# Attention and feed-forward block: first tokens' norm on VectorE, another order in the k and q products, the first codes loaded two units sooner, the last products by halves of a block

## The chip, the core and the metric

The kernel runs on one core of a Trainium2 chip. The core has five engines that run side by side, each with its own queue of instructions: TensorE (PE, matrix products into PSUM, the accumulation memory), VectorE (DVE), ScalarE (ACT), GpSimd (POOL) and SyncE (SP), which here only issues DMA transfers. PE loads its 128x128 stationary operand with an instruction of its own (PEld), which can run beside the product before. The metric is device time in microseconds (us), the median of several runs.

## The reference

The input x is 16 sequences of 256 tokens with 256 features each, 4096 tokens in all. Two steps follow each other:

```python
x = x + layernorm(attention(layernorm(x)))     # 16 heads of 128 features, causal
x = x + layernorm(ffn(layernorm(x)))           # 2048 hidden features
```

Attention projects the normed tokens to q, k and v with biases, takes a causal softmax over 256 keys, and multiplies by an output matrix. The feed-forward step is gelu(gate) times up, and then a down product; its three weight matrices come as 4-bit codes, two in an integer, with one scale for 32 codes, and have to be unpacked. Everything is float32.

## The kernel before

**Arithmetic.** A product of two float32 matrices is made of three products of a faster form: each operand is split into a high part (a copy rounded to that form) and a low part (what the rounding left), and high x high, low x high and high x low are summed in PSUM. `mm3` (line 353) writes such a group. With two slices of the inner dimension a group has six matmuls. `MOVING_LAST` fixes the order inside a slice: high weights with the high moving operand, low weights with the high moving operand, high weights with the low moving operand. ScalarE makes high parts, VectorE or GpSimd low parts.

**Order of work.** All instructions go through `run` (line 95), which keeps the written order on each engine, and all transfers go through `dma` (line 86) to the one queue of SP, also in written order. So an instruction that waits holds everything written later on its engine. Side work (splitting of weights, unpacking of codes, norms) is written as Python generators. `slot` (line 133) runs one step of the first of them that may run at this place, from six lists in a fixed order; `finish` runs a list to its end.

**Start.** `first_tokens` (line 245) loads the first block of 512 tokens in two halves, measures mean and variance (`ln_stats`, line 155: VectorE sums, and a power of -1/2 on GpSimd), norms the tokens, turns them with eight 128x128 transposes on PE (tile `tpx`, four for each half), and splits them into high (`scalar.copy`) and low (`vector.tensor_tensor`) parts in the tile `xT`. VectorE norms the first half, ScalarE the second. Between these, `w_split` (line 298) splits the first k and q weights. PE does 24 transposes of a constant matrix (tile `warm`, line 937) while the first loads are under way. After `first_tokens` the first two v weights are split, with low parts by GpSimd; both are needed for the first v product, which multiplies by four heads at once.

**Attention.** A unit is one head of one block of 512 tokens; there are 8 blocks and 16 heads, so 128 units. The loop of line 952 is a pipeline: in iteration i it does scores and softmax of unit i+3 (`st_s`, tiles `sc` and `pr`), the k and q products of unit i+4 (`st_qk`, tiles `pk` and `pq`), the way of the softmax through DRAM that transposes it (`hop`, `pt`), the product with v (`pz`), the v product (`pv`) and the output product (`po`). In `st_s` VectorE's list of written work holds one slot between the softmax of the two sequences, from which the unpacking of the feed-forward codes can run. In iterations with even i and head pair g (two units a pair), lines 954 to 965 start other work: at block 0, pair 7 (iteration 14) `f_load` issues the first two transfers of codes and scales (`ld`, tag `raw`), and 24 unpacking jobs (`f_make`, line 598) go onto the list `idle`. Each `f_make` issues the loads for the next one in its second step.

**Feed-forward.** The loop of line 1008 goes over 32 groups: 4 pairs of blocks (1024 tokens) times 8 slices of the hidden dimension. In a group, gate and up are computed with seven products in place of eight (`m1` to `m7`, class `Two`, tiles `pa`, `pd`, `pf`, `pe`). `pd`, `pf` and `pe` share the two PSUM buffers of the tag `sc`. Element-wise work goes onto the list `pending`, in a fixed order for ScalarE and VectorE: add, gelu, multiply, high part, low part, for each of four quarters of the group. `part` (line 830) runs one or two of these operations after each product, and `quarter` (line 841) runs as many as a down product needs. The down products of a group (`st_d`, line 850, tile `pd<-inter,wd`) are written among the products of the next group, six matmuls of 512 tokens each, block 1 first. They add up in four PSUM tiles over the eight groups of a pair of blocks.

**End.** Since the last group has no next one, the loop runs once more for its down products alone. Each of the last two blocks goes through `end_now` (line 897): ScalarE copies the two sums (`oT`), PE turns them by eight transposes (`tpo`), `ln_stats` measures 512 tokens, ScalarE and VectorE norm two tiles of 128 tokens each (`fa`), VectorE adds the residual (`xs`) and SP issues the output in two transfers.

Of the kernel before, what the change touches and what calls it, by code (L numbers as in the profile page):

```python
# [18 lines left out]
P = 128  # L19
# [3 lines left out]
NG = 8  # L23
# [5 lines left out]
def kernel(  # L29
# [215 lines left out]
    def first_tokens():  # L245

        xs = [x_load(x, 0, hf) for hf in range(2)]
        yield V_
        stats = []
        for hf in range(2):  # L250
            stats.append((yield from ln_stats([xs[hf][:, t, :] for t in range(2)])))
        w_split(0, "k")
        xn = wide("xn")
        nb = ln_shift(*stats[1], 2)
        for t in range(2):
            mv, rs = stats[0]
            run(
                nc.vector.tensor_scalar,
                xn[:, t, :], xs[0][:, t, :], mv[:, t, 0:1], rs[:, t : t + 1], ALU.subtract, ALU.mult,
            )  # L260
        for t in range(2):
            ln_apply_act(xn[:, 2 + t, :], xs[1][:, t, :], nb, stats[1][1], t)
        w_split(0, "q")
        xt = XT[1, 0] = work.tile([P, 2, 2, TB], F32R, tag="xT", name="xT", bufs=4)
        for hf in range(2):
            tp = ps.tile([P, 2, S], F32, tag=("pk", "pq")[hf], name="tpx")
            for kt in range(2):
                for t in range(2):
                    run(
                        nc.tensor.transpose,  # L270
                        tp[:, kt, t * P : (t + 1) * P], xn[:, 2 * hf + t, kt * P : (kt + 1) * P], ident,
                    )
            cols = slice(hf * S, (hf + 1) * S)
            hi, lo = xt[:, 0, :, cols], xt[:, 1, :, cols]
            run(nc.scalar.copy, hi, tp)
            run(nc.vector.tensor_tensor, lo, tp, f(hi), ALU.subtract)
        ready.add((1, 0))


# [18 lines left out]
    def w_split(p, n):  # L298

        raw = RAW.pop((p, n)).rearrange("p (k c) -> p k c", k=2)  # L300
        key, done = p, True
        if n == "v":
            key, done = p // 2, p % 2
            w = HALF.pop(key) if done else w_tile(n)
            if not done:
                HALF[key] = w
            wv_ = w_view(w)[:, :, :, (p % 2) * 256 : (p % 2 + 1) * 256]
        else:
            w = w_tile(n)
            wv_ = w_view(w)  # L310
        c = qscale if n == "q" else 1.0
        run(nc.scalar.activation, wv_[:, 0], raw, AF.Copy, scale=c)
        if n in "vo":
            run(nc.gpsimd.tensor_tensor, wv_[:, 1], raw, f(wv_[:, 0]), ALU.subtract)
        else:
            run(nc.vector.scalar_tensor_tensor, wv_[:, 1], raw, c, f(wv_[:, 0]), ALU.mult, ALU.subtract)
        ahead = p + (2 if n == "v" else 1)
        if ahead < NG:
            w_raw(ahead, n)
        if done:  # L320
            W[key, n] = w_view(w)
            late.append((now[0] + 4, w_keep, (key, n, w)))
# [27 lines left out]
    MOVING_LAST = ((0, 0), (1, 0), (0, 1))  # L350
    STATIONARY_LAST = ((0, 0), (0, 1), (1, 0))

    def mm3(o, terms, passes=STATIONARY_LAST, start=True, stop=True, shared=False):

        todo = [(lhs(a), rhs(c)) for lhs, rhs in terms for a, c in passes]
        for i, (lhs, rhs) in enumerate(todo):
            run(
                nc.tensor.matmul, o, lhs, rhs, start=start and i == 0, stop=stop and i == len(todo) - 1, skip_group_check=shared
            )
# [9 lines left out]
    def st_qk(i):  # L369
# [9 lines left out]
        mm3(pk, [(lambda a, kt=kt: wk_[:, a, kt, cols], lambda c, kt=kt: xt[:, c, kt, :]) for kt in range(2)], MOVING_LAST)  # L379
# [7 lines left out]
        K[i] = (kh, kl, kr)  # L387

        pq = ps.tile([P, TB], F32, tag="pq", name="pq")
        mm3(pq, [(lambda a, kt=kt: wq_[:, a, kt, cols], lambda c, kt=kt: xt[:, c, kt, :]) for kt in range(2)], MOVING_LAST)  # L390
# [459 lines left out]
    def st_d(k, bb, dh):  # L850


        if not 0 <= k < NGRP:
            return
        sb, g = divmod(k, NG)
        b = 2 * sb + bb
        w = FW[k, "d"]
        tags = (("po0", "po1"), ("pv", "pz"))[bb]
        if g == 0:
            ACC[b, dh] = ps.tile([P, TB], F32, tag=tags[dh], name="pd")  # L860
        po = ACC[b, dh]
        cols = slice(dh * P, (dh + 1) * P)
        i = [quarter(k, c, bb) for c in range(2)]
        mm3(
            po, [(lambda a, c=c: w[:, a, c, cols], lambda s, c=c: i[c][:, s]) for c in range(2)], MOVING_LAST,
            start=g == 0, stop=g == NG - 1, shared=True,
        )
        if g == NG - 1:
            if sb < NSB - 1:
                if dh == 0:  # L870
                    ACC[b] = back_tile()
                back(ACC[b], dh, po)
                if dh == 1:
                    add((urgent, behind)[bb], end(b, ACC.pop(b)), N_)
            else:
                if dh == 0:
                    ACC[b] = wide("oT").rearrange("p a b -> p (a b)").rearrange("p (h n) -> p h n", h=2)
                run(nc.scalar.copy, ACC[b][:, dh], po)
                if dh == 1:
                    add(urgent, end_now(b, ACC.pop(b), tags), V_)  # L880

    def end(b, tr):
        o = yield from back_load(tr)
# [10 lines left out]
        for hf in range(2):  # L894
            dma(half(out, b, hf), X1[b][hf])

    def end_now(b, oT, tags):

        yield V_
        tp = []  # L900
        for hf in range(2):
            tp.append(ps.tile([P, 2, D], F32, tag=tags[hf], name="tpo"))
            for t in range(2):
                for dh in range(2):
                    run(
                        nc.tensor.transpose,
                        tp[hf][:, t, dh * P : (dh + 1) * P], oT[:, dh, (2 * hf + t) * P : (2 * hf + t + 1) * P], ident,
                    )
        o = [tp[t // 2][:, t % 2, :] for t in range(4)]
        mv, rs = yield from ln_stats(o)  # L910
        nb = ln_shift(mv, rs, 4)
        fa = wide("fa")
        for t in range(2):
            ln_apply_act(fa[:, t, :], o[t], nb, rs, t)
        for t in range(2, 4):
            run(
                nc.vector.tensor_scalar,
                fa[:, t, :], o[t], mv[:, t, 0:1], rs[:, t : t + 1], ALU.subtract, ALU.mult,
            )
        for hf in (1, 0):  # L920
            run(nc.vector.tensor_tensor, X1[b][hf], X1[b][hf], fa[:, 2 * hf : 2 * hf + 2, :], ALU.add)
            dma(half(out, b, hf), X1[b][hf])


    first = first_tokens()
# [26 lines left out]
    for i in range(-4, N + 2):  # L952
        p = i // 2
        odd = i % 2 == 1
        if p >= 0 and not odd and p < len(pairs):
            b, g = pairs[p]
            if g == 0 and b + 1 < NBLK:
                add(urgent, ln1(b + 1), N_)
            if b == 0 and g == 7:
                pieces = [(fg, n) for fg in range(NG) for n in "gud"]  # L960
                f_load(*pieces[0])
                for m, piece in enumerate(pieces):
                    add(idle, f_make(*piece, pieces[m + 1] if m + 1 < len(pieces) else None), V_)
            if b == NBLK - 1 and g == 0:
                add(spare, x_ops(0), N_)
# [39 lines left out]
            part(k, name)  # L1005

    X[0].pop("last")()
    for k in range(NGRP + 1):
        sb, g = divmod(k, NG)
        if k < NGRP:  # L1010
            if g == 2 and sb + 1 < NSB:
                while not {(0, 2 * sb + 2), (0, 2 * sb + 3)} <= ready:
                    step(behind)
                add(spare, x_ops(sb + 1), N_)
            if g == NG - 1:
                for b in (2 * sb, 2 * sb + 1):
                    X1[b] = [x_load(x1d, b, hf, ("pr", "tr")[b % 2]) for hf in range(2)]
        if k > 0:
            parts(k, "m1", "m2")
        st_d(k - 1, 1, 0)  # L1020
# [22 lines left out]

_OUTS = [((NT, D), "float32")]
# [48 lines left out]
```

## Time and profile before

| what | value |
|---|---|
| median of three runs | 1543.86 us (1541.33 to 1545.67) |
| the profiled execution | 1548.52 us; its span in the trace 1546.7 us, the rest lies around it |
| mean granted TensorE clock | 0.991 |
| matmuls and weight loads | 7792 and 7792 |
| one unit in the steady part of the attention | 7.83 to 7.84 us from one `sc` start to the next |
| one group of the feed-forward | 14.96 us (1493.25 to 1508.21 us) |
| first `pk` matmul | at 10.87 us |
| first `sc` matmul | at 16.44 us |
| last matmul of the gate and up products ends | some 0.4 us after 1521.58 us |

How to read it: the profile is one execution with times from the start of its span. In a row of the timeline the first number is the start of the first instruction, the second the time from there to the end of the last one, both in us, and xN says how many follow each other. What stands in brackets is how long the engine sat idle before and what ended that. Rows of matmuls overlap at their ends, since products are pipelined, so for their pace starts are compared. "SPq" rows are the issuing of a transfer and not the transfer itself. A table of windows gives busy time of the engines in a stretch, with the number of instructions, then the granted TensorE clock as a fraction of full speed, the busy share of the DMA engines and GB/s. Nearly all instructions carry line 99, the line of the helper `run`, so tiles' names tell them apart.

### The profile page before, as it was taken

The page shows a single profiled execution, that of the slowest core. Times are in us where ns is not written, and L with a number is a line of the kernel's source. Part 1 is how long each engine was busy: PE and PEld are TensorE (multiplying, and loading weights), DVE is VectorE, ACT ScalarE, POOL GpSimd, SP SyncE. Part 2 cuts the span into 40 slices and gives each one's busy share as a digit, 9 for nine tenths or more (in the row PEclk, how much of TensorE's full clock was granted, in tenths as well). Part 3 has the DMA queues.
Part 4 walks back from the last instruction along what each step waited for, and adds up shares of the span by engine and source line. Part 5 has one row for each costly group of instructions (what it writes and reads, how often), then busy time and mean ns, then how long its engine had stood idle before and what let it go on. Part 6 is the DMA issues. An engine that isn't in the chain of part 4 may idle for free.

```text
span 1546.7 us, 25648 instructions
## 1 busy us (share of the span) xinstructions
PE 1510.8 (98%) x7792; PEld 1281.4 (83%) x7792; DVE 1178.4 (76%) x2944; ACT 1033.0 (67%) x2600; POOL 810.1 (52%) x1017
## 2 busy tenths in 40 slices
PE   8999999999999999999999999989999999999996
PEld 7888888888888888888888888877788878878884
DVE  6875878788788788878777777847777777787765
ACT  6876667767767676676675777656666665665663
POOL 3754669568667767766866866861420330240100
PEclk9999999999999999999999999989999999999999
DMA  8998899989899999899899889975547456655551
GB/s 276 335 310 257 249 303 302 313 293 300 280 293 317 291 310 296 267 326 309 266 315 294 287 281 322 324 238 204 216 179 275 185 220 212 236 192 214 218 195 42
DMA packets 200411, 407.55 MB, mean 263 GB/s; under 512 B 21457, under 2 KB 128465, under 8 KB 189521
## 3 DMA queue, kind: packets, MB, share of 16 engines
q1 hardware_dynamic: 200272, 405.91, 78.6%
q8 instruction: 62, 1.02, 0.3%
q14 instruction: 77, 0.62, 0.1%
HBM read 294.15 MB, written 111.67 MB: 262 GB/s over the span
## 4 chain that ended last, share of the span: by engine, by line
PE 80%; DMA 6%; DVE 5%; ACT 4%; SPq 2%; issue 1%; POOL 0%; DVEq 0%; POOLq 0%; ACTq 0%
PE pd L99 11%; PE po L99 10%; PE pk L99 10%; PE pv L99 10%; PE pq L99 9%; PE pz L99 9%; PE sc L99 8%; PE pa L99 7%; PE pf L99 5%; DVE sum L99 3%; DMA wo<-wo 2%; PE pe L99 2%; SPq L91 2%; ACT inter L99 1%; DMA hop<-tr 1%
## 5 line engine op out<-in xcount | busy, mean ns | idle before, releaser
L99 POOL TENSOR_SCALAR pr<-pr,rc 128x128 f32<-128x128 f32 (+1 forms) x512 | 251.7, 508 | 80.8 <-DVE rc L99 80.8
L99 POOL TENSOR_TENSOR pl<-pt,ph 128x512 fp32r<-128x512 f32 x128 | 165.3, 1291 | 218.3 <-ACT ph L99 211.8
L99 ACT ACTIVATE pr<-sc,mn 128x128 f32<-128x128 f32 (+1 forms) x512 | 208.9, 421 | 83.1 <-DVE mn L99 81.7
L99 DVE CUSTOM_DVE_ANT_0 sc<-sc,mask 128x128 f32<-128x128 f32 (+1 forms) x512 | 180.7, 373 | 63.5 <-PE sc L99 54.7
L99 PE MATMUL pv<-wv,xT 128*128 128x512 f32 x768 | 208.9, 407 | 0.0
L99 PE MATMUL pd<-inter,wd 128*128 128x512 f32 x768 | 199.5, 393 | 5.2 <-ACT inter L99 4.0
L99 PE MATMUL pk<-xT,wk 128*128 128x512 f32 x768 | 201.5, 398 | 1.6 <-ACT wv L99 1.4
L99 PE MATMUL pq<-xT,wq 128*128 128x512 f32 x768 | 196.4, 391 | 0.0
L99 ACT ACTIVATE zh<-pz,bqk 128x512 fp32r<-128x512 f32 x128 | 88.5, 692 | 160.6 <-PE pz L99 160.6
L99 POOL TENSOR_TENSOR rs<-rs,mhalf 128x4 f32<-128x4 f32 (+1 forms) x33 | 35.1, 1065 | 288.5 <-DVE rs L99 287.2
L99 PEld LDWEIGHTS pd<-inter,wd 128*128 128x128 f32 x768 | 142.3, 188 | 42.5 <-DVE inter L99 7.0
L99 PEld LDWEIGHTS pq<-xT,wq 128*128 128x128 f32 x768 | 144.5, 188 | 32.9
L99 PE MATMUL po<-zh,wo 128*128 128x512 f32 x512 | 160.3, 394 | 8.4 <-DMA wo<-wo 8.4
L99 PEld LDWEIGHTS pk<-xT,wk 128*128 128x128 f32 x768 | 136.5, 190 | 25.5 <-ACT xT L99 1.6
L99 PEld LDWEIGHTS pv<-wv,xT 128*128 128x128 f32 x768 | 135.0, 189 | 23.6
L99 DVE SCALAR_TENSOR_TENSOR zl<-pz,bqk,zh 128x512 fp32r<-128x512 f32 x128 | 95.2, 744 | 76.9 <-ACT zh L99 76.7
L99 ACT COPY part<-pa 128x512 f32<-128x512 f32 x192 | 111.9, 586 | 62.4 <-PE pa L99 59.8
L99 ACT CAST inter<-sum 128x512 fp32r<-128x512 f32 x128 | 80.1, 626 | 101.1 <-DVE sum L99 100.9
L99 DVE TENSOR_TENSOR inter<-sum,inter 128x512 fp32r<-128x512 f32 x128 | 92.1, 720 | 58.9 <-ACT inter L99 56.0
L99 DVE STREAM_TRANSPOSE tr<-pr 128x768 f32<-128x768 f32 x128 | 123.3, 963 | 1.1
L99 PEld LDWEIGHTS po<-zh,wo 128*128 128x128 f32 x512 | 96.1, 189 | 31.1 <-DMA wo<-wo 11.5
L99 DVE SCALAR_TENSOR_TENSOR kl<-pk,bqk,kh 128x512 fp32r<-128x512 f32 x128 | 96.0, 750 | 30.3 <-ACT kr L99 27.1
(139 smaller groups left out, 3792.6 us busy)
## 6 DMA issues: line engine op xcount, KB each, us to landing
hop<-tr SPq DMA_DIRECT2D x512, 96.0 KB
pt<-hop SPq DMA_DIRECT2D x128, 384.0 KB
wk<-wk SPq DMA_DIRECT2D x64, 512.0 KB
wq<-wq SPq DMA_DIRECT2D x64, 512.0 KB
wo<-wo SPq DMA_DIRECT2D x64, 512.0 KB
wu<-fu SPq DMA_DIRECT2D x32, 1024.0 KB
wg<-fg SPq DMA_DIRECT2D x32, 1024.0 KB
wv<-wv SPq DMA_DIRECT2D x56, 512.0 KB
```

The source lines that it names most:

```text
L91: queue[0] = nc.sync.dma_start(dst, src).ins
L99: ins = op(dst, *args, **kw)
```

## The change

It has five parts.

1. In `first_tokens` VectorE norms all four tiles of 128 tokens, and the split of the k weights is written after that; the split of the q weights is written after the tokens' split. PE does three extra transposes of the constant matrix after the first half's transposes and six after the second's, and 30 in place of 24 at the very start. The low part of the very first v weights is made by VectorE in place of GpSimd.
2. In all k and q products the two matmuls with the low part of the tokens stand at the end of the six (`lows_last`).
3. The first codes and scales are loaded at block 0, pair 6 (iteration 12); the unpacking jobs are still added at pair 7.
4. In the last group the seventh product, `m4`, stands before the down product of the group before, and not after it.
5. The extra turn of the loop and `end_now` go. In their place `st_last` first runs everything pending, and then works through four halves of 256 tokens in a pipeline over n: the two down products of half n (six matmuls of 256 tokens each, copied by ScalarE), between them transposes and measuring of half n-1, and then norm, residual and output of half n-2. The norm is one VectorE instruction (turned sum times 1/deviation plus residual) and one ScalarE instruction (add the shift) for each 128 tokens. Outputs are 256 tokens each, for the last half 128.

```diff
 # first_tokens
-        w_split(0, "k")
         xn = wide("xn")
-        nb = ln_shift(*stats[1], 2)
-        for t in range(2):
-            mv, rs = stats[0]
+        for t in range(4):
+            mv, rs = stats[t // 2]
             run(
                 nc.vector.tensor_scalar,
...
-        for t in range(2):
-            ln_apply_act(xn[:, 2 + t, :], xs[1][:, t, :], nb, stats[1][1], t)
-        w_split(0, "q")
+        w_split(0, "k")
...
+            keep_warm(3 + 3 * hf)
             cols = slice(hf * S, (hf + 1) * S)
             hi, lo = xt[:, 0, :, cols], xt[:, 1, :, cols]
             run(nc.scalar.copy, hi, tp)
             run(nc.vector.tensor_tensor, lo, tp, f(hi), ALU.subtract)
+        w_split(0, "q")
 # w_split
-        if n in "vo":
+        if n in "vo" and (p, n) != (0, "v"):
 # mm3, called with lows_last=True for pk and pq
+        if lows_last:
+            todo = [todo[m] for m in (0, 1, 3, 4, 2, 5)]
 # the start
-    for n in range(24):
-        run(nc.tensor.transpose, warm[:, n % 4, :], ident, ident)
+    def keep_warm(count):
+        for n in range(count):
+            run(nc.tensor.transpose, warm[:, n % 4, :], ident, ident)
+
+    keep_warm(30)
 # attention loop
-            if b == 0 and g == 7:
+            if b == 0 and g == 6:
                 pieces = [(fg, n) for fg in range(NG) for n in "gud"]
                 f_load(*pieces[0])
+            if b == 0 and g == 7:
                 for m, piece in enumerate(pieces):
 # feed-forward loop
-    for k in range(NGRP + 1):
+    for k in range(NGRP):
...
         parts(k, "m7", "m3")
+        if k == NGRP - 1:
+            parts(k, "m4")
         st_d(k - 1, 0, 0)
...
-        parts(k, "m4")
+        if k < NGRP - 1:
+            parts(k, "m4")
         st_d(k - 1, 0, 1)
...
     finish(urgent)
+    finish(behind)
+    st_last()
```

The new end, cut to its core (`end_now` and the branch of `st_d` that called it are removed):

```python
def st_last():
    while pending:
        run(*pending.popleft())
    halves = [(bb, hf) for bb in (1, 0) for hf in range(2)]
    def multiply(n, dh):
        ...
        po = ACC[2 * NSB - 2 + bb, dh][:, tok]          # 256 of the tile's 512 columns
        mm3(po, [...], MOVING_LAST, start=False, shared=True)
        run(nc.scalar.copy, oTs[n][:, dh], po)
    def turn_and_measure(n):                            # 4 transposes, ln_stats of 2 tiles
        tp = ps.tile([P, 2, D], F32, tag=("pk", "pq", "sc", "sc")[n], name="tpo", bufs=2 if n > 1 else 1)
        ...
    def apply(n):
        nb = ln_shift(mv, rs, 2)
        for t in range(2):
            run(nc.vector.scalar_tensor_tensor, x1[:, t, :], os[n][t], rs[:, t : t + 1], x1[:, t, :], ALU.mult, ALU.add)
            run(nc.scalar.activation, x1[:, t, :], x1[:, t, :], AF.Identity, bias=nb[:, t : t + 1])
            if n == len(halves) - 1:
                dma(half(out, b, hf)[:, t, :], x1[:, t, :])
        if n < len(halves) - 1:
            dma(half(out, b, hf), x1)
    for n in range(count + 2):
        if n < count: multiply(n, 0)
        if 0 <= n - 1 < count: turn_and_measure(n - 1)
        if n < count: multiply(n, 1)
        if n >= 2: apply(n - 2)
```

More of the change, by code (lines that the diff above doesn't have):

```diff
@@ L251, in first_tokens @@
             stats.append((yield from ln_stats([xs[hf][:, t, :] for t in range(2)])))
-        w_split(0, "k")
         xn = wide("xn")
-        nb = ln_shift(*stats[1], 2)
-        for t in range(2):
-            mv, rs = stats[0]
+        for t in range(4):
+            mv, rs = stats[t // 2]
             run(
                 nc.vector.tensor_scalar,
-                xn[:, t, :], xs[0][:, t, :], mv[:, t, 0:1], rs[:, t : t + 1], ALU.subtract, ALU.mult,
-            )
-        for t in range(2):
-            ln_apply_act(xn[:, 2 + t, :], xs[1][:, t, :], nb, stats[1][1], t)
-        w_split(0, "q")
+                xn[:, t, :], xs[t // 2][:, t % 2, :], mv[:, t % 2, 0:1], rs[:, t % 2 : t % 2 + 1],
+                ALU.subtract, ALU.mult,
+            )
+        w_split(0, "k")
         xt = XT[1, 0] = work.tile([P, 2, 2, TB], F32R, tag="xT", name="xT", bufs=4)
@@ L351, with mm3 @@
     STATIONARY_LAST = ((0, 0), (0, 1), (1, 0))
-    def mm3(o, terms, passes=STATIONARY_LAST, start=True, stop=True, shared=False):
+    def mm3(o, terms, passes=STATIONARY_LAST, start=True, stop=True, shared=False, lows_last=False):
         todo = [(lhs(a), rhs(c)) for lhs, rhs in terms for a, c in passes]
+        if lows_last:
+            todo = [todo[m] for m in (0, 1, 3, 4, 2, 5)]
         for i, (lhs, rhs) in enumerate(todo):
@@ L378, in st_qk @@
         pk = ps.tile([P, TB], F32, tag="pk", name="pk")
-        mm3(pk, [(lambda a, kt=kt: wk_[:, a, kt, cols], lambda c, kt=kt: xt[:, c, kt, :]) for kt in range(2)], MOVING_LAST)
+        mm3(pk, [(lambda a, kt=kt: wk_[:, a, kt, cols], lambda c, kt=kt: xt[:, c, kt, :]) for kt in range(2)], MOVING_LAST, lows_last=True)
         kh = work.tile([P, TB], F32R, tag="kh", name="kh")
@@ L389, in st_qk @@
         pq = ps.tile([P, TB], F32, tag="pq", name="pq")
-        mm3(pq, [(lambda a, kt=kt: wq_[:, a, kt, cols], lambda c, kt=kt: xt[:, c, kt, :]) for kt in range(2)], MOVING_LAST)
+        mm3(pq, [(lambda a, kt=kt: wq_[:, a, kt, cols], lambda c, kt=kt: xt[:, c, kt, :]) for kt in range(2)], MOVING_LAST, lows_last=True)
         qh = work.tile([P, 2, P], F32R, tag="qh", name="qh")
@@ L868, in st_d @@
         if g == NG - 1:
[L869 to L880, printed above, removed]
+            if dh == 0:
+                ACC[b] = back_tile()
+            back(ACC[b], dh, po)
+            if dh == 1:
+                add((urgent, behind)[bb], end(b, ACC.pop(b)), N_)
     def end(b, tr):
@@ L895, in end @@
             dma(half(out, b, hf), X1[b][hf])
[L897 to L902, printed above, removed]
+    def st_last():
+        k = NGRP - 1
+        while pending:
+            run(*pending.popleft())
+        w = FW[k, "d"]
+        halves = [(bb, hf) for bb in (1, 0) for hf in range(2)]
+        oTs, os, stats = {}, {}, {}
+        def multiply(n, dh):
+            bb, hf = halves[n]
+            tok = slice(hf * S, (hf + 1) * S)
+            cols = slice(dh * P, (dh + 1) * P)
+            i = [quarter(k, c, bb) for c in range(2)]
+            po = ACC[2 * NSB - 2 + bb, dh][:, tok]
+            mm3(
+                po, [(lambda a, c=c: w[:, a, c, cols], lambda s, c=c: i[c][:, s, tok]) for c in range(2)], MOVING_LAST,
+                start=False, shared=True,
+            )
+            if dh == 0:
+                oTs[n] = wide("oT").rearrange("p a b -> p (a b)")[:, 0 : 2 * S].rearrange("p (h n) -> p h n", h=2)
+            run(nc.scalar.copy, oTs[n][:, dh], po)
+        def turn_and_measure(n):
+            tp = ps.tile([P, 2, D], F32, tag=("pk", "pq", "sc", "sc")[n], name="tpo", bufs=2 if n > 1 else 1)
+            oT = oTs.pop(n)
             for t in range(2):
@@ L906, in end_now, with measure @@
                         nc.tensor.transpose,
-                        tp[hf][:, t, dh * P : (dh + 1) * P], oT[:, dh, (2 * hf + t) * P : (2 * hf + t + 1) * P], ident,
+                        tp[:, t, dh * P : (dh + 1) * P], oT[:, dh, t * P : (t + 1) * P], ident,
                     )
[L909 to L922, printed above, removed]
+            os[n] = [tp[:, t, :] for t in range(2)]
+            jobs = deque()
+            stats[n] = None
+            def measure():
+                stats[n] = yield from ln_stats(os[n])
+            add(jobs, measure(), V_)
+            finish(jobs)
+        def apply(n):
+            bb, hf = halves[n]
+            b = 2 * NSB - 2 + bb
+            mv, rs = stats.pop(n)
+            nb = ln_shift(mv, rs, 2)
+            x1 = X1[b][hf]
+            for t in range(2):
+                run(
+                    nc.vector.scalar_tensor_tensor,
+                    x1[:, t, :], os[n][t], rs[:, t : t + 1], x1[:, t, :], ALU.mult, ALU.add,
+                )
+                run(nc.scalar.activation, x1[:, t, :], x1[:, t, :], AF.Identity, bias=nb[:, t : t + 1])
[3 more added lines that the diff above has]
+                dma(half(out, b, hf), x1)
+        count = len(halves)
+        for n in range(count + 2):
+            if n < count:
+                multiply(n, 0)
+            if 0 <= n - 1 < count:
+                turn_and_measure(n - 1)
+            if n < count:
+                multiply(n, 1)
+            if n >= 2:
+                apply(n - 2)
     first = first_tokens()
@@ L1007 @@
     X[0].pop("last")()
-    for k in range(NGRP + 1):
+    for k in range(NGRP):
         sb, g = divmod(k, NG)
[L1010 to L1017, printed above, removed]
+        if g == 2 and sb + 1 < NSB:
+            while not {(0, 2 * sb + 2), (0, 2 * sb + 3)} <= ready:
+                step(behind)
+            add(spare, x_ops(sb + 1), N_)
+        if g == NG - 1:
+            for b in (2 * sb, 2 * sb + 1):
+                X1[b] = [x_load(x1d, b, hf, ("pr", "tr")[b % 2]) for hf in range(2)]
         if k > 0:
```

## Prediction

> **What bounds the kernel now.** I read the page's shares first, then the waits of PE, then the timeline at the places where PE waits.
>
> ```profile
> PE 1510.8 (98%) x7792; PEld 1281.4 (83%) x7792; DVE 1178.4 (76%) x2944; ACT 1033.0 (67%) x2600; POOL 810.1 (52%) x1017
> ```
>
> PE is busy 98% of the span. So a change pays only where PE stands still, runs at a lower clock, or has ended. The first stretch is the start:
>
> ```profile
> 1.56 4.98 PEld L99 LDWEIGHTS warm<-ident 128*128 128x128 f32 x24 [1.56 <-POOL ident masks.py:199]
> 8.13 1.35 PE L99 MATMUL tpx<-ident,xn 128*128 128x128 f32 x8 [1.18 <-DVE xn L99]
> 10.87 2.90 PE L99 MATMUL pk<-xT,wk 128*128 128x512 f32 x6 [1.39 <-ACT wv L99]
> 13.56 1.67 PE L99 MATMUL pq<-xT,wq 128*128 128x512 f32 x6
> ```
>
> ```profile
> 11.50:12.50 1.00, 1.00 (x4) 0.81 (x3) 0.00 (x0) 0.00 (x0) 1.00 (x2) 0.50 1.05 424
> ```
>
> PE warms on a constant (24 weight loads in 4.98, 0.21 each), waits twice for the tokens, and the first k product then takes 2.90 us for six matmuls; the window (busy time of PE, PEld, DVE, ACT, POOL, then the clock) shows why, the granted clock is 0.50. The second stretch is where the first codes are unpacked:
>
> ```profile
> 144.89 0.44 SPq L91 DMA_DIRECT2D ld<-in_gp  x1
> 151.73 0.49 DVE L99 TENSOR_SCALAR codes<-ld 128x256 int32<-128x256 int32 x2 [5.90 <-DMA ld<-in_gp]
> 153.40 0.38 PE L99 MATMUL sc<-kl,qh 128*128 128x256 f32 x1 [2.29 <-DVE kl L99]
> 155.24 2.44 PE L99 MATMUL pk<-xT,wk 128*128 128x512 f32 x6
> 163.98 1.56 PE L99 MATMUL pk<-xT,wk 128*128 128x512 f32 x6
> ```
>
> VectorE stands 5.90 us before the codes that were asked for at 144.89; behind it in its queue is `kl`, for which PE waits 2.29 us, and the next products are slow (2.44 against the usual 1.56 us; the clock was 0.50 from 155 to 157 us). The third is the end:
>
> ```profile
> 1524.52 3.97 PE L99 MATMUL pd<-inter,wd 128*128 128x512 f32 x15 [1.19 <-ACT inter L99]
> 1526.48 0.59 ACT L99 COPY oT<-pd 128x512 f32<-128x512 f32 x1 [2.01 <-PE pd L99]
> 1527.85 0.59 ACT L99 COPY oT<-pd 128x512 f32<-128x512 f32 x1 [0.78 <-PE pd L99]
> 1528.33 0.63 ACT L99 ACTIVATE sum<-sum 128x512 f32<-128x512 f32 x1
> 1530.39 1.23 PE L99 MATMUL pd<-inter,wd 128*128 128x512 f32 x3 [1.90 <-ACT inter L99]
> 1541.67 1.29 DVE L99 TENSOR_TENSOR xs<-xs,fa 128x512 f32<-128x512 f32 x2
> ```
>
> The last quarter's gelu (1528.33) is queued on ScalarE behind two copies that wait for PE, and PE waits for that quarter. Then two blocks are measured and normed one after the other, to 1542.96.
>
> **The change, part by part.** *Start (part 1).* VectorE has `rs` of the first half at 6.04 (power on GpSimd 5.32 to 6.04) and of the second at 7.02. A norm instruction starts 0.35 after the one before (two take 0.73), so with its wait four run 6.25 to 7.82, against 8.87 when ScalarE ended the second half. The k low part (0.69) moves behind them, to 8.45; only `pk` needs it. PE: 24 warm transposes pace 0.21 us; six more end near 7.6 (0.21 at first, then the 0.13 of eight `tpo` in 1.03). Each four transposes take 0.5: first half 7.6 to 8.1, three warm ones to 8.5, second half to 9.0, six warm ones to 9.75. ScalarE copies the second half 9.17 to 9.75 (0.52 each), VectorE has the low parts at 9.5 and 10.4, so `pk` starts at 9.8 in place of 10.87, and without the idle stretches that preceded the clock of 0.50, its six take 1.36, ending 11.15 in place of 13.77 (with drain). q weights: ScalarE 9.75 to 10.35, VectorE to 11.08; `pq` needs the low ones at 11.36 and ends 12.5. v weights: ScalarE to 10.95 and 11.5; GpSimd makes one low part in place of two (2.51 for two), 11.55 to 12.8. `pv` (1.47 by starts) needs that at its second matmul, 12.73, so it ends near 14.0 and `sc` starts there in place of 16.44. **-2.4 us.** VectorE's extra 0.69 for v ends at 11.75, before `kl` can start; without that cover it would cost its 0.69. SP: `rawv` for later pairs moves from 10.51 to about 11.1, behind a DMA queue that ran at 0.7 to 1.1 shares to 18.75; its reader moved from 17.12 to 14.7, so up to 0.5 may be lost there. Bounds: `sc` can't start before `qr` at 13.5, -2.9. If the clock stays at half, 39 transposes and eight of the tokens at 0.21 put `pk` at 11.7 and its end at about 14.5, +0.7.
>
> The Trainium skill, "TensorE: Matmul & The Clock Gate", Part 4: PE-mode transpose, says that transposes don't count as PE being busy, so that the full clock is not engaged by them; that speaks against warming with transposes. Here they went from 0.21 to about 0.13 us each between 6.7 and 8.5 us with nothing but transposes on PE, which disagrees; by the rule the sum below would be -9.4, by the rows it is -12.5.
>
> *Order of the k and q matmuls (part 2).* Count and weight loads stay, 7792 for 7792. Matmuls of 512 columns start 0.232 apart in `pk`, 0.228 in `pq`, 0.227 in `po`, and 0.235 in `pv`, the only one in another order. Fastest and slowest of these rows as ends: (0.232+0.228-2x0.227)x6x128 = -5 to (2x0.235-0.460)x6x128 = +8 us. I take 0, since `pk` and `pq` themselves are the nearest rows and differ by 0.004 with one order. The earlier low weights (second slice, fourth in place of fifth) are made units ahead.
>
> *First codes (part 3).* From 150.61 to 162.82 the unit takes 12.21 in place of 7.84: 4.37 lost. The two issues (0.44 and 0.78 on SP) move to about 128.7, after the weight copies of iteration 11, where SP has nothing until the `pt` load at 133.78, and their `raw` buffer held the fourth output weights, read at 88.82, so SP isn't held. The landing took 6.8 us; from 128.7 that gives 136, ten before the reader at 145.8. 0.25 MB more at 128.7 take some 0.8 us of DMA time at 302 GB/s; the `hop` writes ahead (125.76) are issued by then and `pt` follows 5 us later. **-4.4 us**; no more can be won. If another transfer is late next, nothing is won: PE's other attention waits are for `wo` (8.4 us in six), so 0 is the other end.
>
> *End (parts 4 and 5).* The earlier `m4` needs the PSUM buffers of `m5`, which VectorE frees at 1519.3 and 1520.5: PE loses 0.2 and 0.5, but waits afterwards anyway. VectorE's order stays; the last quarter but one is multiplied at 1523.65, ScalarE rounds it to 1524.3, and now gelu (to 1524.95), multiply (1525.6), high part (1526.3) and low part (1527.0) follow at once, 3.9 us sooner than before (1530.39 for the high part, here 1526.3). The first half's products run from 1524.35, stand for the low part to 1525.05 and end at 1526.3 (256-column matmuls start 0.12 apart, as in `pz`; 48 take 5.6, as 24 of 512 took 5.4). Copies stand behind the high part: 0.37 each (`qr`'s pace) to 1526.65, 1527.0. Transposes to 1527.75. VectorE for each half: two sums 0.67, two means 0.2, one `rs` 0.15; shift 0.1, two norms 0.8 (`ql`: 0.40 apart): 1.9. In the written order (measure 1, norm 0, measure 2, ...) with the transposes' times: measures end 1528.8, 1530.8, 1532.75, 1534.85, norms 1531.7, 1533.65, 1535.75; the last waits for GpSimd's power (0.72, to 1535.6) and ends 1536.65. ScalarE's last add (0.45) ends at 1537.2, where before the last residual ended at 1542.96: -5.7; the last transfer has half the bytes, which I count at nothing. **-5.7 us.** Bounds: -6.0 with that transfer's 128 KB saved; if each half's power on GpSimd is exposed, 4 x 0.75 come back: -2.7.
>
> Sum: -2.4 + 0 - 4.4 - 5.7 = -12.5 us. On the profiled execution that is 1548.5 - 12.5 = 1536.0. The median lies 4.7 below that execution; 1543.86 - 12.5 = **1531.4 us**, 0.8% less.
>
> **Rivals.** (a) The clock is not held at the start: +0.7 in place of -2.4, 1534.5 us. For it: the clock fell to 0.50 at 10.5 though PE had worked 1.35 of the 3.5 us before, and one trace can't say how much work holds it. Against: in the working above PE has no gap over 0.2 us from 1.56 to 12.7. (b) The codes come in time, but another late transfer takes their place: 1535.8. For it: DMA shares of 0.92 around 145 us. Against: the load is moved to an emptier place, and nothing is added. (c) The end is bound by exposed waits: 1534.4. For it: GpSimd's 0.72 sits between every measure and norm. Against: another half's work is written between them. (d) Slower: the new order in all 256 k and q groups costs what `pv` shows, 1.47 us by starts for its six in place of 1.39 and 1.37: 0.18 x 128 = +23, 1554 us; it decides from 0.13 us a unit, 11 ns a matmul, where the gain and the 0.3% (4.6 us, about what a measurement here can tell) are used up. For it: `pv` is the one group in another order. Against: `pv`'s excess is mostly its first start (0.31), which follows the plain float32 products of `pz`. At `pv`'s inner pace only (+8) the result is 1539.4, about the same as before. (e) The change of order does nothing: that is my forecast for it.
>
> **How the numbers follow.** The forecast 0.60, (a) 0.12, (b) 0.10, (c) 0.06: all faster, 0.88. The inner pace of `pv`: 0.06, same. (d) 0.06, slower. Range: from the best ends (-2.9, -4.4, -6.0: 1530.6) less the 2.5 by which the lowest run lies under the median and some of the order's gain, 1526.5; up to two rivals together, 1539.0.
>
> **What would show it.** Right: `pk` starts near 9.8 with about 1.4 us for its six and clock 1.00 through 13; `sc` first at 14.0; no VectorE wait for `ld` near 145 and units of 7.83 through it; `pk` and `pq` starts still 0.23 apart; gelu of the last quarter near 1524.3 less the shift of 6.8, and 12.9 us from there to the last output's issue. Wrong: a clock of 0.50 after 10 us, a VectorE or PE wait of over 2 us between 140 and 165, unit length off 7.83, or VectorE idle for over 1 us between measures.

## The result, and the profile after

The changed kernel takes 1531.47 us (median of four runs, 1527.93 to 1532.69); the kernel before took 1543.46 us beside it. The ratio is 0.9918, with a 95% interval of 0.9896 to 0.9941: 0.8% less, 12.0 us by the medians and 12.7 by the ratio. The profiled execution took 1532.46 us, its span 1530.7 us, so it lies 1 us above its median where that of before lay 4.7 above; of the 16.0 us between the two spans some 4 are a matter of which execution was profiled, as will be seen.

**The page's shares** of the kernel after. PE is as busy as before, in a shorter span:

```profile
PE 1505.6 (98%) x7831; PEld 1279.9 (84%) x7831; DVE 1178.0 (77%) x2950; ACT 1033.0 (67%) x2606; POOL 809.1 (53%) x1018
```

**The start**, timeline of the kernel after (start, time to the end of the group, engine, what, and in brackets the idle time before; rows between these are left out):

```profile
1.56 6.20 PE L99 MATMUL warm<-ident 128*128 128x128 f32 x30 [1.56 <-POOL ident masks.py:199]
5.82 0.73 DVE L99 TENSOR_SCALAR xn<-xs,mv,rs 128x256 f32<-128x256 f32 x2
7.60 0.60 PE L99 MATMUL tpx<-ident,xn 128*128 128x128 f32 x4
9.69 1.62 PE L99 MATMUL pk<-xT,wk 128*128 128x512 f32 x6
11.15 1.52 PE L99 MATMUL pq<-xT,wq 128*128 128x512 f32 x6
13.97 0.38 PE L99 MATMUL sc<-kr,qr 128*128 128x128 f32 x2
16.57 0.63 ACT L99 ACTIVATE wv<-rawv 128x512 fp32r<-128x512 f32 x1 [1.81 <-DMA rawv<-in_wv]
21.57 0.49 PE L99 MATMUL sc<-kr,qr 128*128 128x128 f32 x2 [2.19 <-ACT qr L99]
```

The first k product starts at 9.69 (forecast 9.8) and takes 1.62 us in place of 2.90; the first scores start at 13.97 (forecast 14.0, before 16.44). The line at 16.57 is what the forecast made too small: ScalarE stands 1.81 us for the third v weights. The last line is what that costs PE: ScalarE makes `qr` of the second unit later, and PE waits 2.19 us for it. In the kernel before it was:

```profile
22.62 0.49 PE L99 MATMUL sc<-kr,qr 128*128 128x128 f32 x2 [0.77 <-ACT qr L99]
```

By the eighth k group (a k group is the six `pk` matmuls of a unit), 57.24 us before and 56.46 after, 0.8 us of the 2.5 are left.

**The first codes**, from the same view. SP issues the load at 127.91 between two other transfers, and VectorE finds it there:

```profile
127.91 0.47 SPq L91 DMA_DIRECT2D ld<-in_gp  x1
...
133.00 0.32 SPq L91 DMA_DIRECT2D pt<-hop  x1
```

```profile
144.89 0.15 DVE L99 RECIPROCAL rc<-sm 128x2 f32<-128x2 f32 x1
144.96 0.48 DVE L99 TENSOR_SCALAR codes<-ld 128x256 int32<-128x256 int32 x2
```

No bracket stands behind the codes any more. The scores of the units there start at 142.00, 149.83 and 157.66, 7.83 us apart, where one unit took 12.21.

**The end**:

```profile
1514.08 0.63 ACT L99 ACTIVATE sum<-sum 128x512 f32<-128x512 f32 x1
...
1514.95 2.50 PE L99 MATMUL pd<-inter,wd 128*128 128x256 f32 x16 [0.22 <-DVE inter L99]
1515.53 0.62 ACT L99 CAST inter<-sum 128x512 fp32r<-128x512 f32 x1 [0.83 <-DVE sum L99]
1516.06 0.75 ACT L99 COPY oT<-pd 128x256 f32<-128x256 f32 x2
...
1525.04 0.70 POOL L99 TENSOR_TENSOR rs<-rs,mhalf 128x2 f32<-128x2 f32 x1 [1.27 <-DVE nb L99]
1525.39 1.92 ACT L99 ACTIVATE xs<-xs,nb 128x256 f32<-128x256 f32 x4 [1.03 <-DVE xs L99]
1525.77 0.16 DVE L99 SCALAR_TENSOR_TENSOR nb<-mv,rs 128x2 f32<-128x2 f32 x1
```

The last quarter's gelu (1514.08) now comes ahead of the copies. From it to the end of ScalarE's last addition (1525.39 + 1.92 = 1527.31) it takes 13.2 us (forecast 12.9). From the start of the last `pf` products to the end of the span it is 23.1 us, where it was 29.0.

### The profile page after: what moved, and what is told of

It is laid out like the page before. It is cut to its first block, busy times and chain, and to the rows that moved or that the text cites. A ratio compares the mean times of both kernels' runs of the same rounds, so it can differ in the third digit from the quotient of the medians.

```text
span 1530.7 us, 25745 instructions
## 1 busy us (share of the span) xinstructions
PE 1505.6 (98%) x7831; PEld 1279.9 (84%) x7831; DVE 1178.0 (77%) x2950; ACT 1033.0 (67%) x2606; POOL 809.1 (53%) x1018
## 4 chain that ended last, share of the span: by engine, by line
PE 85%; DVE 5%; ACT 4%; DMA 3%; issue 1%; SPq 1%; POOL 0%; POOLq 0%; ACTq 0%; DVEq 0%
PE pd L99 11%; PE po L99 11%; PE pv L99 11%; PE pk L99 10%; PE pq L99 10%; PE pz L99 9%; PE sc L99 9%; PE pa L99 7%; PE pf L99 5%; DVE sum L99 3%; PE pe L99 2%; DMA wo<-wo 2%; ACT inter L99 1%; SPq L91 1%; DVE inter L99 1%
## 5 line engine op out<-in xcount | busy, mean ns | idle before, releaser
L99 PE MATMUL pd<-inter,wd 128*128 128x512 f32 (+1 forms) x792 | 199.8, 386 | 2.5 <-DVE inter L99 1.4
L99 PEld LDWEIGHTS po<-zh,wo 128*128 128x128 f32 x512 | 96.0, 189 | 29.2 <-DMA wo<-wo 9.6
```

What stands on the lines that cost most here:

```text
L99: ins = op(dst, *args, **kw)
```

## The experiments

Each run came with a trace. Four marks are compared in them, each from the starts of groups of matmuls in the timeline: when the eighth k group starts; what is lost at the codes (from the start of the 16th k group to that of the 23rd, less seven units of 7.83 us); what is lost from the 23rd to the 128th k group (less 105 such units); and the end, from the start of the last `pf` group to the end of the span. All in us.

| kernel | eighth k group | lost at the codes | lost 23rd to 128th | end |
|---|---|---|---|---|
| before | 57.24 | 4.9 | 8.1 | 29.0 |
| before, once more | 58.48 | 2.2 | 3.4 | 29.0 |
| before, part 1 (start) | 55.56 | 3.2 | 5.3 | 29.0 |
| before, part 2 (order) | 57.41 | 6.9 | 5.4 | 29.3 |
| before, part 3 (codes) | 59.04 | 0.5 | 4.4 | 29.2 |
| before, parts 4 and 5 (end) | 57.30 | 4.2 | 1.7 | 23.3 |
| before, pending work first | 57.14 | 4.3 | 2.6 | 26.5 |
| after | 56.46 | 0.5 | 3.8 | 23.1 |
| after, once more | 54.58 | 0.5 | 4.2 | 23.1 |
| after, `m4` back | 55.10 | 0.5 | 3.2 | 23.2 |
| after, pending work not first | 55.59 | 0.5 | 2.9 | 26.9 |
| after, no fill-in transposes | 55.74 | 0.5 | 3.3 | 23.1 |
| after, copies of weights later | 55.01 | 0.4 | 4.2 | 23.1 |
| that, and output weights sooner | 54.72 | 0.6 | 6.4 | 23.4 |

Four of these kernels ran only once, beside one run of before at 1545.95 us: before with pending work first (1539.60), after with `m4` back (1530.55), after with pending work not first (1534.44) and after without fill-in transposes (1530.46). Of them only the traces are read.

### Each part alone

Four kernels, measured together, against 1544.67 us for the kernel before. The diffs are the five parts of the change as shown above, the last two together. A time is a median; the difference given with a ratio follows from the ratio.

Part 1, the start:

> The kernel before with part 1 alone (the start). In the trace after, the first scores began 2.47 us sooner, but from the third k group on only 1.06 and from the eighth on 0.78 us were left, while ScalarE waited 1.81 us for the third v weights. Theory: that wait belongs to part 1, so here too the eighth k group starts about 0.8 us sooner than before (56.5 against 57.24 us) and ScalarE waits 1.5 to 2 us for rawv before 17 us. Rival: part 1 is worth its 2.4 us by itself and the other parts took it back; then the eighth k group starts near 54.8 us. Time: -0.8 or -2.4 us, which the interval can hardly tell apart.

Measured: 1540.89 us, ratio 0.9972 (0.9958 to 0.9985), 4.3 us less. The eighth k group starts at 55.56 us and ScalarE waits for the weights here too, though less:

```profile
15.56 0.63 ACT L99 ACTIVATE wv<-rawv 128x512 fp32r<-128x512 f32 x1 [0.49 <-DMA rawv<-in_wv]
```

So the wait belongs to part 1, and its length differs from execution to execution: 1.81, 1.18, 1.50 and 1.89 us in four traces with the new start, 2.12 in one without its fill-in transposes, 0.49 here. PE's wait for the second unit's `qr` goes with it: 2.19, 1.54, 1.88, 2.25, 2.48 and here 0.82 us. Neither number expected for the eighth group (56.5 or 54.8) came out; it lies between.

Part 2, the order of the k and q products:

> The kernel before with part 2 alone (low parts of the tokens last). Theory: no change, within 2 us of before; k and q groups keep starts 0.23 us apart and a unit keeps 7.83 us. Rivals: the pace of other groups comes with the order, -5 us at the fastest row and +8 us at the slowest, units of 7.79 or 7.90 us.

Measured: 1542.00 us, ratio 0.9977 (0.9966 to 0.9987), 3.6 us less. The trace gives no reason for it: the median distance from one k group to the next is 7.833 us, as in the kernel before and after, neighbouring `pk` matmuls start 0.234 us apart in all three (median between 230 and 1000 us), and each takes what it took. Both lines are from the view of the tile `pk` between 240 and 340 us (durations in ns, shortest, median, longest), first of before, then of this kernel:

```profile
L99 PE MATMUL pk<-xT,wk x78: 387/396/398, 243.5 to 338.7; 128*128 128x512 f32 x78
```

```profile
L99 PE MATMUL pk<-xT,wk x74: 387/396/398, 245.6 to 339.9; 128*128 128x512 f32 x74
```

Part 3, the codes:

> The kernel before with part 3 alone (first codes two units sooner). Theory: the 5.90 us wait of VectorE and the 2.29 us wait of PE go, the unit from 150.6 us takes 7.83 in place of 12.21 us, and the time is 4.4 us less. Rival: another late transfer takes the place, a wait of 2 us or more of VectorE or PE between 140 and 170 us, and the gain is under 2 us.

Measured: 1539.75 us, ratio 0.9965 (0.9953 to 0.9977), 5.4 us less. Every k group from 145.69 to 169.19 starts 7.83 us after the one before:

```profile
145.69 1.56 PE L99 MATMUL pk<-xT,wk 128*128 128x512 f32 x6
153.52 1.56 PE L99 MATMUL pk<-xT,wk 128*128 128x512 f32 x6
161.35 1.56 PE L99 MATMUL pk<-xT,wk 128*128 128x512 f32 x6
```

In the six traces without part 3 the wait of VectorE for the codes is there each time, but not of one length: 5.90, 4.74, 5.17, 5.23, 5.72 and 6.63 us, and the stretch loses 2.2 to 6.9 us in place of 0.5.

Parts 4 and 5, the end:

> The kernel before with parts 4 and 5 alone (the end). Theory: from the last group's first product to the end of the span 5.8 us less, and nothing else; time 5.8 us less. Rival: 3 us less or nothing, if the waits at GpSimd's power show in VectorE between the measures.

Measured: 1535.59 us, ratio 0.9944 (0.9930 to 0.9958), 8.6 us less. The end takes 23.3 us in place of 29.0, as expected. VectorE has no wait over 1 us between the measures, so the powers are covered.

Together the four ratios make 21.9 us (the medians 20.5), where the whole change makes 12. That could not be left so, and led to the next two runs.

### The kernels before and after, unchanged, against the kernel before

> The kernel before, unchanged, measured against itself. The four parts alone came out 4.3, 3.6, 5.4 and 8.6 us faster, 21.9 us together, where the whole is 12 us, and the order of the k and q products had nothing in its trace that is worth 3.6 us. Theory: runs of one kernel differ by 1 to 5 us through waits for output weights between the 23rd and the 128th unit (lost there: 8.1 us in the first profile of before, 1.7 to 5.4 in the other traces), and the intervals are too narrow for it; then this run can differ from 1.000 by up to 0.2%, and loses under 6 us in that stretch in its profile. Rival: the kernel before loses more there in every execution and any edit takes that away; then this run is at 1.000 within 0.1% and loses 7 us or more in that stretch.

Measured: 1541.93 us beside 1543.68, ratio 0.9987 with an interval from 0.9977 to 0.9997. The same program against itself thus comes out 2 us faster, with an interval that leaves out 1. The trace stands with the first theory: 3.4 us are lost from the 23rd k group on, against 8.1 in the first profile of before. A half of these losses and more are waits of PE for output weights. Waits of PE, the whole execution (who waits for whom, us in total, times, longest), first of the first profile of before, then of this run:

```profile
PE po L99 <- DMA wo<-wo: 8.4, 6, 4.1
```

```profile
PE po L99 <- DMA wo<-wo: 7.0, 5, 5.2
```

Within 170 to 1000 us it was 4.3 us in one and 1.9 in the other. A single unit, the 107th, loses 4.1 of the 8.1 us in the first profile: PE waits there, and then the granted clock is 0.50 between 847 and 850 us. So a difference of 2 us between two kernels, or an interval that just misses 1, tells nothing here. If each part carries the same 2 us, which is not shown, 2.3, 1.6, 3.4 and 6.6 are left, together 13.9 us. What made the runs called before the slower half of identical pairs is not settled.

> The kernel after, unchanged, once more, beside the same runs of before. Theory: the sum of the local differences in the traces, -1.7 at the start (eighth k group), -4.2 at the codes, -5.9 at the end, is 11.8 us, and the measured difference is 10 to 14 us; the stretch from the 23rd to the 128th unit loses 3 to 4.5 us. Rival: the sum of the parts measured alone holds, 18 to 22 us.

Measured: 1531.18 us, ratio 0.9930 (0.9909 to 0.9952), 12.5 us by the medians and 10.8 by the ratio; 4.2 us lost from the 23rd group on. The local differences, not the sum of the parts measured alone, agree with the whole.

### Where the end's 5.8 us come from

First the kernel before, with pending work run first:

```diff
         if k > 0:
             parts(k, "m1", "m2")
+        while k == NGRP and pending:
+            run(*pending.popleft())
         st_d(k - 1, 1, 0)
```

> The kernel before with one thing of the new end: at the extra turn of the loop everything pending is run before the last down products. Theory: the last quarter's gelu no longer stands behind two copies that wait for PE, PE's wait of 1.90 us before that quarter goes, and from the last gate and up product to the end of the span it takes 2 us less, since the two blocks are still measured and normed one after the other; so the halves bring the other 3.8 us. Rival: the queueing of the gelu is the whole of it, and it takes 5 us or more less; or the halves are all of it, and it takes under 0.5 us less.

Measured: the end takes 26.5 us, 2.5 less. PE now runs 18 products in a row behind one wait, and the copies stand behind the last high part:

```profile
1518.06 4.66 PE L99 MATMUL pd<-inter,wd 128*128 128x512 f32 x18 [1.19 <-ACT inter L99]
```

```profile
1517.92 0.63 ACT L99 ACTIVATE sum<-sum 128x512 f32<-128x512 f32 x1
1519.37 0.62 ACT L99 CAST inter<-sum 128x512 fp32r<-128x512 f32 x1 [0.83 <-DVE sum L99]
1520.02 0.59 ACT L99 COPY oT<-pd 128x512 f32<-128x512 f32 x1
```

The other way round, the kernel after without the first step of its end:

```diff
-        while pending:
-            run(*pending.popleft())
         w = FW[k, "d"]
```

> The kernel after, where the last part does not run everything pending first; each half's products run what they need. Theory: the last quarter's gelu falls behind the first four copies on ScalarE, the third half's products wait for it, VectorE stands idle for over 1 us, and the end is 2 us later. Rival: VectorE's measures and norms cover it, under 0.5 us.

Measured: the end takes 26.9 us, 3.8 more than with it, and more than the 2 expected. ScalarE's gelu stands behind four copies again (1516.76), and VectorE stands 2.71, 0.91 and 1.28 us before the measures:

```profile
1516.49 0.37 ACT L99 COPY oT<-pd 128x256 f32<-128x256 f32 x1 [0.78 <-PE pd L99]
1516.76 0.63 ACT L99 ACTIVATE sum<-sum 128x512 f32<-128x512 f32 x1
```

So running pending work first is worth 2.5 us in the old end and 3.8 in the new; the halves (with part 4) are worth 2.0 without it (29.0 to 26.9) and 3.4 with it (26.5 to 23.1). Each is worth more beside the other.

Part 4 by itself, the earlier seventh product:

```diff
-        if k == NGRP - 1:
-            parts(k, "m4")
         st_d(k - 1, 0, 0)
         slot(V_)
         slot(A_ + G_)
-        if k < NGRP - 1:
-            parts(k, "m4")
+        parts(k, "m4")
```

> The kernel after without part 4: the last group's seventh product stands behind the down product again. Theory: nothing, 0 to 0.3 us later at the end, since VectorE's order of work up to the last products is the same and sets their start. Rival: the earlier product was what brought the last quarter forward; then 1.4 us later.

Measured: the end takes 23.2 us in place of 23.1, a difference that the marks can't tell from nothing (23.1 to 23.4 in the six other traces with the new end and pending work first). In the kernel after PE pays for the earlier place with two waits for the buffers, as forecast but shorter: 0.1 us before the first row (the `pf` matmuls end at 1509.09) and 0.24 before the second:

```profile
1509.19 0.73 PE L99 MATMUL pe<-xh,wg 128*128 128x512 f32 x2
...
1510.39 0.73 PE L99 MATMUL pe<-xh,wu 128*128 128x512 f32 x2 [0.24 <-DVE sum L99]
```

### What holds the clock at the start

```diff
-            keep_warm(3 + 3 * hf)
-    keep_warm(30)
+    keep_warm(24)
```

> The kernel after without the fill-in transposes: 24 at the start, none between. Theory: the clock falls to 0.50 within 9 to 14 us as it did before, the first k and q groups take 1 to 2 us longer and the first scores start at 14.5 to 15.5 in place of 13.97 us; but the eighth k group starts within 0.4 us of 56.46, since ScalarE waits for the third v weights to 16.5 anyway. Rival: the fill-in is not what holds the clock: it stays at 1.00 without it and the first scores start at 13.97 or sooner.

Measured: the rival is right in this execution. Without the fill-in the clock stays at 1.00 through the first products and scores, the first scores start at 13.11, and the eighth k group at 55.74, in the middle of what the new start gives with fill-in (54.58 to 56.46). Timeline and windows (busy time of PE, PEld, DVE, ACT, POOL, then the clock) of this kernel:

```profile
1.56 4.42 PE L99 MATMUL warm<-ident 128*128 128x128 f32 x24 [1.56 <-POOL ident masks.py:199]
6.22 1.87 PE L99 MATMUL tpx<-ident,xn 128*128 128x128 f32 x8 [0.24 <-DVE xn L99]
8.84 1.63 PE L99 MATMUL pk<-xT,wk 128*128 128x512 f32 x6 [0.75 <-ACT xT L99]
```

```profile
9.50:10.50 1.00, 1.00 (x6) 0.82 (x5) 1.00 (x2) 0.79 (x2) 0.13 (x1) 1.00 0.86 143
10.50:11.50 1.00, 1.00 (x6) 0.80 (x5) 0.14 (x1) 0.99 (x2) 1.00 (x1) 1.00 1.06 420
```

The gaps are 0.24 and 0.75 us; in the kernel before they were 1.18 and 1.39, and in its second trace 2.05 and 1.01, with first k products of 2.90 us in both. In all six traces with the old start the clock falls to 0.50 between 9 and 11 us; in none of the eight with the new one does it fall before 21 us. The earlier norm shortens the gaps; the fill-in then adds nothing that shows. There is one execution without it; another might need it.

The clock falls later, though, and behind the wait for the third v weights. PE stands 2.48 us for `qr` here, then the clock is 0.50 from about 22 to 25 us, and the third k group takes 2.76 us:

```profile
21.01 0.49 PE L99 MATMUL sc<-kr,qr 128*128 128x128 f32 x2 [2.48 <-ACT qr L99]
...
22.68 2.76 PE L99 MATMUL pk<-xT,wk 128*128 128x512 f32 x6
```

Two kernels with the fill-in show the same fall at the same place (`m4` back, after PE's wait of 1.88 us, and pending work not first, 2.25); the two traces of the kernel after don't (2.19 and 1.54). So it is not the missing fill-in, nor the length of the wait alone.

The six further constant transposes at the very start seem to cost time where the clock opens late. In the first trace of the kernel after, PE is still busy with them at 7.6 us, while VectorE norms the first half from 5.82 to 6.55; in its second trace the 30 take 4.99 us in place of 6.20, the tokens' transposes start at 6.38 and the first k product at 8.77:

```profile
6.38 0.63 PE L99 MATMUL tpx<-ident,xn 128*128 128x128 f32 x4
```

### The third v weights, and a faster version

```diff
-            late.append((now[0] + 4, w_keep, (key, n, w)))
+            late.append((now[0] + (5 if p == 0 else 4), w_keep, (key, n, w)))
```

This moves the copies of the first k and q weights to DRAM from before the loads of the third and fourth v weights to behind them.

> The kernel after, where the copies of the first k and q weights to DRAM (512 KB each) are issued behind the loads of the third and fourth v weights and not ahead of them. Theory: those copies stand ahead of the v weights in the DMA queues; without them the weights land by 14.5 us in place of 16.57, ScalarE's wait of 1.81 us goes and the eighth k group starts at about 55.0 in place of 56.46 us: 1.4 us less. Rival: the landing is set by the loads issued before both, or by the issue at 11.3 us; then ScalarE still waits over 1.2 us and the gain is under 0.5 us.

Measured: 1529.64 us, ratio 0.9904 (0.9885 to 0.9923) against 1544.18 for before. ScalarE's wait is gone. Timelines of SP and of ScalarE in this kernel:

```profile
11.17 0.93 SPq L91 DMA_DIRECT2D rawv<-in_wv  x2
12.15 0.42 SPq L91 DMA_DIRECT2D wk<-wk  x1
```

```profile
14.43 0.58 ACT L99 CAST vh<-pv 128x512 fp32r<-128x512 f32 x1 [0.61 <-PE pv L99]
14.91 0.64 ACT L99 ACTIVATE wv<-rawv 128x512 fp32r<-128x512 f32 x1
```

The loads are issued at 11.17 us, about as in the kernel after (11.30), and land by 14.91 in place of 16.57, so it was the two copies ahead of them in the one queue and not their issue. The next kernel has the same order, and ScalarE doesn't wait there either. PE's wait for the second unit's `qr` is 0.77 us again, as in the kernel before. From the second to the third k group it takes 6.34 us in place of 7.75, the expected 1.4 less (7.1 to 8.4 in the five traces of the kernel after and its three variants above); the eighth starts at 55.01. The granted clock reads 0.95 for nearly all of this trace, where it is 1.00 in the others, but `pk` matmuls start 0.23 us apart and units 7.833 as there, so the comparison stands. In the time of the whole kernel 1.4 us can't be told from the kernel after.

The last run loads the output weights one unit sooner as well, since PE's waits for them are the largest that are left:

```diff
         if odd:
             weights((p + 4, "k"), (p + 4, "q"))
+            if p + 1 >= NG:
+                weights((p + 1, "o"))
         else:
-            weights((p, "o"), (p + 4, "v"))
+            if p < NG:
+                weights((p, "o"))
+            weights((p + 4, "v"))
```

> The kernel of the run before this, and from block 1 on the output weights of a pair are loaded one unit sooner (behind the k and q weights of the iteration before). Theory: PE's waits for wo (7.6 us in four, one of 5.08 at the end of the attention, and the lower clock after them) are late issues; they fall under 2 us and the time by 5 to 9 us against the kernel of the run before. Rival: SP now waits for the last product of the pair before, the transfers written behind it come later, PE waits for the transposed softmax instead and the time is the same or more.

Measured: 1526.88 us, ratio 0.9883 (0.9863 to 0.9903), the fastest kernel of this study, and the smallest time of it (1525.40). Every wait for output weights is gone, but half of the gain went into new ones, as the rival had it: PE now waits for the transposed softmax. Waits of PE in this kernel:

```profile
PE sc L99 <- ACT qr L99: 2.8, 5, 1.1
PE pz L99 <- POOL pl L99: 2.1, 4, 0.8
...
PE pz L99 <- ACT ph L99: 1.4, 1, 1.4
```

Against the run before it is 2.8 us less by the medians, not the 5 to 9 expected, and the intervals of the two overlap. Around the end of the attention 4.5 us were won (from the 128th k group to the last `pf` group 501.8 us in place of 506.3), and between the 23rd and the 128th 2.2 were lost (6.4 against 4.2), most of it in one place, where the chain of work that ended last runs through a late `hop` transfer (the 107th unit loses 3.5 us there):

```profile
834.48 4.26 DMA hop<-tr
```

## Why the prediction was right, point by point

The forecast was 1531.4 us, and 1531.47 was measured. That the two agree to 0.1 us is luck: the terms were not all right (the start too large by 0.6 and the codes by 0.7 us by the traces' middles), and the kernel differs from itself by 2 us.

- **The start, -2.4.** Right up to the first scores in the profiled execution: `pk` at 9.69, scores at 13.97, the clock at 1.00. That these agree to 0.1 us is luck too: in the other traces with the new start the first scores come between 13.04 and 14.28, with the old start between 16.36 and 17.75. Mis-sized behind them: the forecast allowed "up to 0.5" for the third v weights and put nothing of it into the sum, and ScalarE stood 0.5 to 2.1 us for them. The eighth k group is at 57.35 us in the middle of the six traces with the old start and at 55.56 in the middle of the five with the new one (fill-in and order of copies unchanged): -1.8. The run with the copies moved shows the cause: two copies of 512 KB ahead in the queue. The forecast named the busy queue and the later issue (0.6 us), but not which transfers stood ahead of the load.
- **The clock.** The forecast put the clock of 0.50 down to the idle stretches. That fits all fourteen traces, old start and new, but no run lengthened the gaps alone. It put the new start's full clock partly down to fill-in transposes, which the run without them did not bear out. The Trainium skill's rule ("TensorE: Matmul & The Clock Gate", Part 4: PE-mode transpose) that transposes don't count as work for the clock is not seen here. With nothing but transposes on PE, the warm-up's starts are 0.213 us apart at first and 0.110 later (the forecast took 0.13): the change comes at 4.8 us in the run without fill-in (24 in 4.42 us), at 5.9 in the second trace of before (24 in 4.91), and only behind the 24th in the first trace of before (5.38). The column of the granted clock says 1.00 there all along, so the pace alone shows it.
- **The order, 0.** Right: 7.833 us from one k group to the next, and 0.234 from one `pk` matmul to the next, in either order. Neither `pv`'s pace nor its 1.47 us came with it.
- **The codes, -4.4.** The mechanism is right, and so is the place of the new load (127.91, forecast 128.7) and that nothing takes the wait's place. The size is that of one execution: over six traces the stretch loses 2.2 to 6.9 us, 4.2 in the middle, against 0.5: -3.7. "No more can be won" was wrong, since it took one execution's stall for the stall.
- **The end, -5.7.** Right: 29.0 to 23.1, -5.9 by the traces' middles. Part 4 costs its two waits for buffers and brings nothing that can be told (0.1). Running pending work first and the halves with part 4 bring 2.5 and 3.4 in this order. GpSimd's powers are covered, the last one too: it runs from 1525.04 to 1525.74 while VectorE norms the half before (1524.88 to 1525.75), and VectorE goes on at 1525.77.
- **The sum.** -1.8 + 0 - 3.7 - 5.9 = -11.4 by the traces' middles, -12.0 and -12.5 by the medians. The spans of the two profiles differ by 16.0: 0.8 up to the eighth k group, 4.4 at the codes, 4.3 from the 23rd to the 128th, 0.7 from there to the last `pf` group and 5.8 at the end. The 4.3 belong to no part of the change: the profile of before lost 8.1 us there, its second trace 3.4. The forecast's choice, to work out the change on one execution and take it off the median, avoided that.
- **The rivals.** (a), a clock not held at the start, did not come, though a fall behind the third v weights did in three traces. (b), another late transfer in the place of the codes, did not come; a late transfer of another kind, the third v weights, took part of the start's gain. (c), exposed waits, and (d), the slower order, did not come.

## What to carry to other kernels

When a step is moved forward, look up what lies ahead in the DMA queue of each load that it brings nearer: a load can be issued in time and land late behind a copy that nobody needs soon, and writing the load ahead of the copy took that wait away here. On an engine with a fixed order, run the element-wise work that a product waits for ahead of the copies that wait for products, above all at the end: here that was worth 2.5 us in the old end and 3.8 in the new one. And measure a kernel against itself before parts of a change are priced by time: here the same program differed by 2 us from itself with an interval that left out 1, and only the marks in the traces priced the parts.

## What was not expected

The stall at the first codes is one event of the program, and its loss differs by three times between executions (2.2 to 6.9 us); the losses from the 23rd to the 128th unit, a large share of them waits for output weights, differ still more (1.7 to 8.1 us). Four edits in separate places each came out faster by more than their traces show, 21.9 us together where the whole is 12. The comparison of the kernel with itself would account for 2 us of that in each part, if each part carries them; a reason for those 2 us was not found.
